# A four-layer graph network on one core: layer 0 with the adjacency as TensorE's weights

## The chip, the core and the metric

The kernel runs on one core of a Trainium2 chip, in one launch. The metric is the device time of that launch in microseconds. A core has TensorE (matmuls, out of weights that are loaded ahead of each of them, into PSUM), VectorE (DVE), ScalarE (ACT) and GpSimd (POOL), and queues that issue DMA transfers; here the SyncE queue (SP) issues nearly all of them.

## The reference, cut to what matters

A graph of 4096 nodes has features x (4096 x 64) and a dense float32 adjacency `adj` (4096 x 4096) of zeros and ones, 67 MB. Four layers follow one another, each as `x = layernorm(x + layer(x, adj))`. Layers 1 and 3 are hyperbolic attention over all pairs of nodes, layer 2 a decayed sum over each node's last neighbours. The change is in layer 0:

```
deg = clip(sum(adj, axis=1) + 1, 1)
h_neigh = (adj @ X + X) / deg
z = concat([X, h_neigh], axis=1) @ W + b          # W: 128 x 64
out = relu(z);  out = out / max(norm(out), 1e-12)
x = layernorm(x + out)
```

So z is X W_top + b + ((adj + I) X W_bottom) / deg: multiplying by W_bottom can come after the sum over neighbours or before it.

## The kernel before, in words

The host lays the adjacency out as (group of target nodes, source node within its block, block of source nodes, target node). There are four groups of 1024 targets (`GROUPS`, worked from 3 down to 0) and 32 blocks of 128 source nodes (`BLOCKS`, 31 down to 0). `load` (L712) brings two blocks for one group: 128 x 2048 float32, 1 MB, into one of six buffers. As the entries are 0 or 1, the upper half of each float32 is the same number in bfloat16; `edge` is that view, with a step of two elements. Every layer streams the adjacency again, 64 loads each.

*Layer 0, before.* `parts_of` (L1489 to L1492) splits x into three bfloat16 parts whose sum is x: two of 64 columns each side by side in `first`, the last in `third` together with a column of ones. For each block of source nodes, these parts are TensorE's weights (128 or 65 columns), and the edges are the moving operand, 512 targets at a time (L1602): four matmuls per block, so eight per load. The sums have features on partitions and targets along the row, in four PSUM banks of a group: two for `first`, two for `third`. The identity term is added by 16 small matmuls per group (L1611). At the end of a group the four accumulators are copied to SBUF, L1628 and L1636, on ScalarE (for the last group two of them on VectorE). `end_0` then multiplies them in float32 by W_bottom with the three parts added up (L1541 by `sum_w`, L1546 by `count_w`, which also passes the count of neighbours); this turns targets onto partitions. After that come the division by the degree (L1551 to L1553), the node's own part (L1554), relu (L1558), squares on POOL (L1560) and the norm (L1562 on). The own part x W_top + b is computed by `linear` (transposes L1396, a copy L1401, products L1407) and `own_part` (L1527), one group later.

*Checks.* `check` (L876) on VectorE makes sure that a load holds zeros and ones alone; it reads the whole load and so holds its buffer. In layer 0 between five and seven of the 16 loads of a group are checked, the others in layer 2.

*Order of the work.* Work per group that isn't the big stream (ends of groups, norms, preparation of the next layer's operands in `norm_rows` and `prepare`) is written as Python generators, "row work". `tick(n)` advances a counter and emits those steps of the queues whose due count has come; `later` puts a generator into a queue, and `yield n` asks for n ticks. `need(tag)` emits steps until a tag is done. So a step's place in the program is set by ticks. In layers 0 and 2 the order on TensorE and ScalarE is the program's (`manual_schedule`), elsewhere the tile scheduler chooses the order by readiness that it estimates, within what `in_order` (a dependency without a semaphore) fixes. `mark` ties row work behind the last pair instruction of its engine, but not while `anchored[0]` is false, as it is in the first group of a layer.

*Layer 1 and 3.* `attend` works one group against all 32 blocks, two blocks to a load. For each block: six matmuls into a z tile of two PSUM banks (L1170, L1173, L1176), a sigmoid (L1133) and a square (L1190) on ScalarE, a product on VectorE (L1193); for each two blocks a second product on VectorE (L1196) and eight float32 passes on TensorE (L1148). There are three z tiles, in the banks that layer 0's accumulators had. In the first pass of layer 1 (group 3), the row work of the last group of layer 0 (group 0) runs beside the pairs, much of it on POOL: L1560, the inverse roots (L784 to L795), L1566 and L1567, then `norm_rows` from L929.

Of the kernel before, what the change touches and what calls it, by code (L numbers as in the profile page):

```python
# [10 lines left out]
F32 = mybir.dt.float32  # L11
F16 = mybir.dt.float16
I32 = mybir.dt.int32
BF16 = mybir.dt.bfloat16
# [5 lines left out]
P = 128  # L20
# [41 lines left out]
def gnn_stack_kernel(  # L62
# [4 lines left out]
    weights: bass.AP,  # L67
    small: bass.AP,
# [14 lines left out]
    given_b = const.tile([P, 2 * D + 3], F32, name="given_b")  # L83
    nc.scalar.dma_start(given, small[:, : 2 * D + 3])
# [479 lines left out]
    def stream(fits):  # L564

        with ExitStack() as st:
# [307 lines left out]
            def check(s, g, a, junk):  # L874
                n = s * (NB // 2) + g
                V.scalar_tensor_tensor(  # L876
                    junk, a, 0.0, a, ALU.not_equal, ALU.not_equal, accum_out=odd[:, n : n + 1]
                )
# [247 lines left out]
            def sigmoid(layer, s, j):  # L1126
# [6 lines left out]
                nc.scalar.activation(sig, left_bs[s], AF.Sigmoid, bias=right[:, j : j + 1])  # L1133
                return sig

            def attend(layer, s, rate, then):
# [4 lines left out]
                lag = []  # L1141
# [14 lines left out]
                for g in reversed(range(NB // 2)):  # L1156
# [4 lines left out]
                    for k in (1, 0):  # L1161
# [27 lines left out]
                        sig = ahead_of.pop() if ahead_of else sigmoid(layer, s, j)  # L1189
                        nc.scalar.activation(  # L1190
                            sq[:, k], zp, AF.Square, bias=ROOT + OFF, scale=-1.0 / UNIT
                        )
                        V.scalar_tensor_tensor(ts[k][:, k], zp, 0.0, sig, ALU.max, ALU.mult)  # L1193
                        tick(rate)
# [194 lines left out]
            def linear(layer, s, weights, finish):  # L1389

                for h in range(2):
                    xt = row.tile([P, W], F32, name="x_t")[:D]
                    yield from free()
                    t = take(F32, P, W)
                    for k in range(SB):
                        nc.tensor.transpose(  # L1396
                            t[:D, k * P : (k + 1) * P],
                            x_of(layer)[:, s * WB + h * SB + k, :], ident,
                        )
                    yield near()  # L1400
                    nc.scalar.copy(xt, t[:D])  # L1401
                    held.pop()
                    yield near()
                    yield from free()
                    t = take(F32, P, SB, D)
                    for k in range(SB):
                        nc.tensor.matmul(  # L1407
                            t[:, k, :], xt[:, k * P : (k + 1) * P], weights, start=True, stop=True
                        )
                    yield near()  # L1410
                    finish(slice(s * WB + h * SB, s * WB + (h + 1) * SB), t)
                    held.pop()
                    yield 1

# [55 lines left out]
            with ExitStack() as lp:  # L1470
                own = lp.enter_context(tc.tile_pool(name="m0_own", bufs=1))
                ps = lp.enter_context(tc.tile_pool(name="m0_ps", bufs=6, space=PSUM))
# [5 lines left out]
                first = own.tile([P, NB, 2 * D], BF16, name="first")  # L1478
                third = own.tile([P, NB, D + 1], BF16, name="third")
                xw = halves.bitcast(F32)  # L1480
                sum_w = keep.tile([P, D + 1], F32, name="sum_w")
                count_w = keep.tile([D + 1, D + 1], F32, name="count_w")
                ident_b = own.tile([P, P], BF16, name="ident_b")

                def parts_of(s):

                    at, rest = blocks(s), grp("w_att")
                    nc.sync.dma_start(x0[:, at, :], x_in[:, at, :])
                    V.tensor_copy(first[:, at, :D], x0[:, at, :])  # L1489
                    V.tensor_sub(rest, x0[:, at, :], first[:, at, :D])  # L1490
                    V.tensor_copy(first[:, at, D:], rest)  # L1491
                    V.tensor_sub(third[:, at, :D], rest, first[:, at, D:])  # L1492

                def constants():
# [10 lines left out]
                    V.memset(sum_w[:, D:], 0.0)  # L1505
                    V.tensor_copy(sum_w[:D, :D], weights_sb[:D, 1])
                    V.tensor_copy(sum_w[D:, :D], w0_sb[D:, :])
                    V.memset(count_w, 0.0)
                    V.memset(count_w[D:, D:], 1.0)
                    V.tensor_copy(count_w[:D, :D], sum_w[:D, :D])  # L1510
# [8 lines left out]
                V.memset(third[:, :, D : D + 1], 1.0)  # L1519
                parts_of(GROUPS[0])  # L1520
# [4 lines left out]
                def own_part(at, t):  # L1525

                    V.tensor_add(xw[:, at, :], t, b0_sb[:, None, :].to_broadcast([P, SB, D]))  # L1527

                def end_0(s, tops):
                    z = grp("z0")  # L1530
                    yield from free()

                    for some in ((0, 1),) if spare else ((0,), (1,)):
                        ts = []
                        for h in some:
                            top, low = tops[h]
                            t = take(F32, P, SB, P)
                            for k in range(SB):
                                cols = slice(k * P, (k + 1) * P)
                                to = t[:, k, : D + 1]  # L1540
                                one = nc.tensor.matmul(  # L1541
                                    to, top[:, cols], sum_w, start=True, stop=False
                                )
                                if place[0] == 1 and not k:
                                    in_order(one.ins, pairs_last[mybir.EngineType.PE])
# [392 lines left out]
```

## Time and profile before

| | us |
|---|---|
| median of three runs | 1046.84 (1044.62 to 1047.78) |
| the profiled execution | 1045.84 |
| its span, first to last instruction | 1043.7 |
| first layer-0 matmul | 9.33 |
| last two layer-0 matmuls (L1602) begin | 173.41 |
| first pair matmul of layer 1 (L1170) | 177.12 |
| first L1196 of layer 1's first pass | 183.97 |
| first L1196 of its second pass | 273.96 |

The granted TensorE clock is 0.986 of full speed on average.

In a timeline line the columns are: start, duration, engine, line of the kernel, operation, output and input by the program's names, shapes, how many instructions are merged, and in brackets the idle time before it with what ended that. PE is TensorE's matmuls, PEld its loads of weights. A float32 matmul shows as two instructions (two passes).

### The profile page before, as it was taken

To read this page: it belongs to the slowest core of one execution; us is meant where nothing else is said; L and a number is where in the kernel's file an instruction comes from. 1 tells how busy PE (TensorE), PEld (TensorE's weight loads), DVE (VectorE), ACT (ScalarE), POOL (GpSimd) and SP (SyncE) were. 2 spreads that over 40 slices of the span, in tenths; PEclk is the share of its full clock that TensorE was granted. 3 is DMA by queue.
4 is the path that set the end of the run, shared out by engine and by line. 5 is a ranking of instruction groups with operands and counts; after the bars stand their busy time and mean duration, and the time that the engine had idled before them with its cause. 6 is when DMAs were issued, how large, how long until landed. Compare 5 with 4: busy or idle time off the path is not lost.

```text
span 1043.7 us, 13511 instructions
## 1 busy us (share of the span) xinstructions
PE 969.8 (93%) x4759; PEld 397.0 (38%) x4845; DVE 906.7 (87%) x1404; ACT 751.8 (72%) x872; POOL 332.5 (32%) x695
## 2 busy tenths in 40 slices
PE   6899999899999999999999999998999999999991
PEld 2455455333333333333333344443333333333320
DVE  7485876799999999999489489979999999999996
ACT  0103125679989898898677688898998898888960
POOL 0011111471066256266111020105402652562660
PEclk9999999899999999999999999999999999999996
DMA  9999999655675566566599999995565665665600
GB/s 370 420 413 421 369 421 421 230 174 189 223 249 214 202 235 212 197 237 216 227 346 349 374 348 322 317 335 197 201 218 192 237 241 194 243 219 200 214 8 17
DMA packets 38242, 271.62 MB, mean 260 GB/s; under 512 B 4242, under 2 KB 4371, under 8 KB 5396
## 3 DMA queue, kind: packets, MB, share of 16 engines
q1 hardware_dynamic: 37728, 270.03, 70.3%
q8 instruction: 40, 0.66, 0.2%
q10 hardware_dynamic: 436, 0.63, 0.2%
q14 instruction: 38, 0.31, 0.1%
HBM read 269.58 MB, written 1.05 MB: 259 GB/s over the span
## 4 chain that ended last, share of the span: by engine, by line
PE 56%; DVE 15%; POOL 5%; ACT 4%; issue 2%; ACTq 0%; POOLq 0%; DVEq 0%
PE acc L1148 16%; PE z L1790 11%; PE z L1173 7%; PE z L1176 7%; PE z L1170 7%; DVE t L1196 7%; DVE t L1193 6%; PE z L1802 3%; PE z L1756 2%; ACT sq L1190 1%; ACT sq L1797 1%; PE aux L1279 1%; PE aux L1114 1%; ACT sig L1133 1%; POOL rb L969 0%
## 5 line engine op out<-in xcount | busy, mean ns | idle before, releaser
L1193 DVE SCALAR_TENSOR_TENSOR t<-z,sig 128x1024 f32<-128x1024 f32 x255 | 307.3, 1217 | 17.2 <-ACT sq L1190 15.0
L1190 ACT ACTIVATE sq<-z 128x1024 f32<-128x1024 f32 x256 | 255.2, 1023 | 59.2 <-PE z L1176 27.8
L1196 DVE SCALAR_TENSOR_TENSOR t<-sq,t 128x2048 f32<-128x2048 f32 x127 | 294.4, 2318 | 0.3
L1133 ACT ACTIVATE sig<-left_b,right 128x1024 f32<-128x1024 f32 x255 | 286.1, 1150 | 10.4 <-DVE t L1193 6.2
L1148 PE MATMUL acc<-t,xe 128*64 128x512 f32 x1024 | 255.9, 609 | 11.7 <-DVE t L1196 11.4
L1173 PE MATMUL z<-lo_hi,hi_lo 128*128 128x512 f16 x512 | 194.2, 379 | 3.6 <-issue 0.7
L1176 PE MATMUL z<-dst,src 74*128 74x512 f16 x512 | 195.3, 381 | 0.0
L1170 PE MATMUL z<-edges,two_i 128*128 128x512 bf16 x462 | 181.4, 393 | 7.8 <-DVE t L1193 5.6
L1797 ACT ACTIVATE sq<-z 128x512 bf16<-128x512 f32 (+1 forms) x192 | 138.1, 740 | 39.4 <-PE z L1790 38.5
L1148 PEld LDWEIGHTS acc<-t,xe 128*64 128x64 f32 x1024 | 64.0, 136 | 141.3 <-issue 105.8
L876 DVE SCALAR_TENSOR_TENSOR t<-edges 128x2048 bf16<-128x2048 f32 x41 | 94.0, 2308 | 18.8 <-DMA edges<-in_adj_dram 18.8
L1170 PEld LDWEIGHTS <-two_i 128*128 128x128 bf16 x512 | 50.2, 98 | 120.8 <-issue 74.7
L1602 PE MATMUL acc<-edges,first 128*128 128x512 bf16 x241 | 76.9, 395 | 16.9 <-DVE first L1491 9.3
L1790 PE MATMUL z<-edges,pass_by 128*128 128x512 bf16 x241 | 84.8, 388 | 6.7 <-ACT sq L1797 5.8
L1790 PE MATMUL z<-edges,enter 128*128 128x512 bf16 x247 | 85.4, 387 | 0.4
L1602 PE MATMUL acc<-edges,third 128*65 128x512 bf16 x256 | 79.7, 392 | 0.6
L1176 PEld LDWEIGHTS <-src 74*128 74x128 f16 x512 | 49.2, 96 | 72.4 <-issue 10.9
L1173 PEld LDWEIGHTS <-hi_lo 128*128 128x128 f16 x512 | 50.3, 98 | 62.9 <-issue 17.4
L876 DVE SCALAR_TENSOR_TENSOR junk<-edges 128x2048 bf16<-128x2048 f32 x23 | 52.5, 2284 | 15.0 <-DMA edges<-in_adj_dram 15.0
L1296 POOL TENSOR_TENSOR w_att<-x,u 128x512 f32<-128x512 f32 x6 | 16.2, 2706 | 149.4 <-ACT u L1290 149.4
L1401 ACT COPY x_t<-aux 64x512 f32<-64x512 f32 x8 | 4.6, 576 | 64.4 <-PE aux L1396 64.4
L1560 POOL TENSOR_TENSOR sq<-z 128x512 f32<-128x512 f32 x4 | 10.0, 2491 | 122.2 <-DVE z L1558 101.5
(477 smaller groups left out, 1034.5 us busy)
## 6 DMA issues: line engine op xcount, KB each, us to landing
edges<-in_adj_dram SPq DMA_DIRECT2D x256, 1024.0 KB, 5.0
x<-in_x_dram SPq DMA_DIRECT2D x4, 256.0 KB, 8.8
out_dram<-x ACTq DMA_DIRECT2D x2, 256.0 KB, 2.4
out_dram<-x SPq DMA_DIRECT2D x2, 256.0 KB, 2.4
weights_sb<-in_weights_dram ACTq DMA_DIRECT2D x1, 96.0 KB, 6.2
given<-in_small_dram ACTq DMA_DIRECT2D x1, 0.5 KB
xw<-in_small_dram ACTq DMA_DIRECT2D x1, 2.0 KB
```

Of the source, the lines that this page charges most:

```text
L876: V.scalar_tensor_tensor(junk, a, 0.0, a, ALU.not_equal, ALU.not_equal, accum_out=odd[:, n : n + 1])
L1133: nc.scalar.activation(sig, left_bs[s], AF.Sigmoid, bias=right[:, j : j + 1])
L1148: it = nc.tensor.matmul(acc[h * D : (h + 1) * D, :], xe[:, j, :], t[:, k, h * W : (h + 1) * W], start=j == BLOCKS[0], stop=j == BLOCKS[-1],)
L1170: nc.tensor.matmul(half, two_i, edge[:, at : at + W], start=True, stop=False)
L1173: nc.tensor.matmul(half, hi_lo[:, of], lo_hi[:, to], start=False, stop=False)
L1176: last = nc.tensor.matmul(half, src[:, of], dst[:, to], start=False, stop=True)
L1190: nc.scalar.activation(sq[:, k], zp, AF.Square, bias=ROOT + OFF, scale=-1.0 / UNIT)
L1193: V.scalar_tensor_tensor(ts[k][:, k], zp, 0.0, sig, ALU.max, ALU.mult)
L1196: V.scalar_tensor_tensor(t, sq, HIGH**2, t, ALU.add, ALU.mult)
L1602: nc.tensor.matmul(accs[h][:m], lhs[:, j, :], edge[:, at : at + W], start=j == BLOCKS[0], stop=j == BLOCKS[-1],)
L1790: nc.tensor.matmul(z[:, h : h + W], lhs, rhs[:, h : h + W], start=j == BLOCKS[0], stop=True, skip_group_check=True,)
L1797: weighed[0] = nc.scalar.activation(w, z[:, :n], AF.Exp, bias=-(OFF_EDGE + CUT) * LN2, scale=-LN2)
```

## The change

W_bottom is applied before the sum over neighbours. For each half group (four blocks), `turn` transposes x, and the new `parts_of` multiplies it by a 65 x 128 matrix `enter_w` that the host puts together (W_bottom beside W_top, with b as its last row against a row of ones). The first 64 columns of the product are split into three bfloat16 parts, and these lie side by side with a column of ones in `parts`, 193 columns; the other 64 are the own part `xw`. Then the two operands change places: a 128 x 128 piece of the edges is TensorE's weights, and the 193 columns are the moving operand. A load takes 16 matmuls of 193 columns, each with its own weights. The sums have targets on partitions, two blocks of targets to a bank, four banks to a group, six banks in rotation (`BANKS`). At the end of a group VectorE adds the three parts up from PSUM and takes reciprocals of the counts. `linear`, `own_part`, `sum_w`, `count_w`, the copies of the accumulators and the float32 products of `end_0` go.

x comes in four pieces within the first loads (`fetch`) rather than one per group. Some orders are fixed by hand: the checks of the first group behind the first split, the split of the second layer's weights behind the second one, the norm's reduce of the last group behind the last pair operation, and four sigmoids of the first pass behind squares. The last group's `end_0` waits in ticks of other counts.

```diff
+    enter_w = const.tile([D + 1, 2 * D], F32, name="enter_w")
+    nc.scalar.dma_start(enter_w, enter_in)
...
-                nc.scalar.activation(sig, left_bs[s], AF.Sigmoid, bias=right[:, j : j + 1])
+                one = nc.scalar.activation(sig, left_bs[s], AF.Sigmoid, bias=right[:, j : j + 1])
+                if 1 < len(squares) < 6:
+                    in_order(one.ins, squares[-2].ins)
...
+                def turn(h):
+                    t = bank(4).rearrange("p b f -> p (b f)")
+                    for k in range(SB):
+                        nc.tensor.transpose(
+                            t[:D, k * P : (k + 1) * P], x0[:, h * SB + k, :], ident
+                        )
+                    nc.scalar.copy(x_ts[h % 2][:D], t[:D])
...
+                    for k in range(SB):
+                        nc.tensor.matmul(
+                            t[:, k, :], x_ts[h % 2][:, k * P : (k + 1) * P], enter_w,
+                            start=True, stop=True,
+                        )
+                    rest = grp("w_att")[:, :SB, :]
+                    hi, mid, lo = (parts[:, at, n * D : (n + 1) * D] for n in range(3))
+                    V.tensor_copy(hi, t[:, :, :D])
+                    V.tensor_sub(rest, t[:, :, :D], hi)
+                    nc.scalar.copy(xw[:, at, :], t[:, :, D:])
+                    V.tensor_copy(mid, rest)
+                    split.append(V.tensor_sub(lo, rest, mid))
...
+                def end_0(s, total, deg):
+                    z, pooled = grp("z0"), s == GROUPS[-1]
+                    yield 2 if pooled else 1
+                    V.tensor_mul(z, total, over(deg))
+                    V.tensor_add(z, z, xw[:, blocks(s), :])
                     V.tensor_scalar(z, z, 0.0, None, ALU.max)
                     sq, n2 = grp("sq"), nums("n2")
                     nc.gpsimd.tensor_mul(sq, z, z)
-                    yield 1
-                    V.tensor_reduce(n2, sq, AX.X, ALU.add)
+                    yield 2 if pooled else 1
+                    one = V.tensor_reduce(n2, sq, AX.X, ALU.add)
+                    if pooled:
+                        in_order(one.ins, pairs_last[mybir.EngineType.DVE])
...
-                                for lhs, accs, m in parts:
-                                    for h in range(2):
-                                        at = k * WW + h * W
-                                        nc.tensor.matmul(
-                                            accs[h][:m], lhs[:, j, :], edge[:, at : at + W],
-                                            start=j == BLOCKS[0], stop=j == BLOCKS[-1],
-                                        )
+                            for i in range(WB):
+                                for k in (1, 0):
+                                    j = 2 * g + k
+                                    at = k * WW + i * P
+                                    nc.tensor.matmul(
+                                        banks[i // 2][:, i % 2, :PARTS], edge[:, at : at + P],
+                                        parts[:, j, :PARTS],
+                                        start=j == BLOCKS[0] and i % 2 == 0, stop=j == BLOCKS[-1],
+                                        skip_group_check=True,
+                                    )
...
+                        for q in (0, 2, 3, 1) if last else range(4):
+                            acc = banks[q]
+                            at = slice(2 * q, 2 * q + 2)
+                            V.tensor_reduce(
+                                total[:, at],
+                                acc[:, :, : 3 * D].rearrange("p b (c d) -> p b d c", c=3),
+                                AX.X, ALU.add,
+                            )
+                            V.reciprocal(deg[:, at], acc[:, :, 3 * D])
                         if not last:
-                            later(end_0(s, tops))
-                        if s > 0:
-                            own_of = linear(0, s - 1, w0_sb[:D, :], own_part)
-                            later(in_turn((0, s - 1), own_of))
+                            later(end_0(s, total, deg))
...
-                        later(end_0(GROUPS[-1], tops), False, 4)
+                        later(end_0(GROUPS[-1], total, deg))
```

## The prediction

> **What bounds the kernel now.** I read the page first (busy shares, then the 40 slices), then windows of 4 us over layer 0, the queue's own waits, and the timelines of TensorE, ScalarE and VectorE around the step from layer 0 to layer 1. The first two pieces are from the page, the third from the windows (us; PE, PEld, DVE, ACT, POOL busy; clock; DMA share; GB/s), the fourth from the DMA queue's waits between 60 and 175 us (sum, times, longest).
>
> ```profile
> PE 969.8 (93%) x4759; PEld 397.0 (38%) x4845; DVE 906.7 (87%) x1404; ACT 751.8 (72%) x872; POOL 332.5 (32%) x695
> ...
> DMA  9999999655675566566599999995565665665600
> ```
>
> ```profile
> 88.00:92.00 4.00, 3.84 (x28) 2.18 (x28) 0.20 (x1) 2.36 (x4) 0.00 (x0) 1.00 0.99 414
> ...
> 116.00:120.00 4.00, 3.94 (x20) 1.81 (x19) 3.93 (x19) 0.00 (x0) 0.00 (x0) 1.00 0.90 344
> 120.00:124.00 4.00, 4.00 (x32) 2.27 (x31) 3.83 (x11) 1.35 (x3) 0.00 (x0) 1.00 0.89 326
> ```
>
> ```profile
> SPq L712 <- DVE junk L876: 50.1, 15, 5.8
> ```
>
> A slice is 26.1 us, and the seven full slices of DMA are layer 0. There 64 loads of 1.05 MB arrive at 421 GB/s, 2.49 us each. TensorE looks full, but its work on a load is 8 matmuls at 0.226 us, 1.8 us; it is not the bound of this stage. What layer 0 loses is at most the dip between 112 and 132 us: 365, 344, 326, 334 and 397 GB/s where 421 is possible, worth (56+77+95+87+24) x 4 / 421 = 3.2 us. VectorE is full there, still working off its checks (L876, 2.28 us, which hold the load's buffer) and row work.
>
> After layer 0, pairs (layers 1 and 3) take 4.6 us for two blocks on VectorE (2 x 1.14 + 2.2) and nearly that on TensorE. From the step itself, TensorE:
>
> ```profile
> 173.86 0.61 PE L1030 MATMUL aux<-ident,ys 128*128 128x128 f16 x8
> ...
> 177.12 0.39 PE L1170 MATMUL z<-edges,two_i 128*128 128x512 bf16 x1 [2.21 <-ACT w_att L1636]
> ...
> 179.76 0.33 PE L1541 MATMUL acc<-sum_w,sums 128*128 128x65 f32 x2
> ...
> 183.28 0.39 PE L1170 MATMUL z<-edges,two_i 128*128 128x512 bf16 x1
> ```
>
> TensorE stands 2.21 us until ScalarE has emptied the accumulators, does two blocks of pairs, and then spends 3.52 us on the 32 float32 passes of `end_0`. VectorE, same region:
>
> ```profile
> 179.97 1.23 DVE L1193 SCALAR_TENSOR_TENSOR t<-z,left_b 128x1024 f32<-128x1024 f32 x1 [4.62 <-ACT sq L1190]
> 181.70 0.18 DVE L1551 RECIPROCAL deg<-acc 128x4 f32<-128x4 f32 x1 [0.50 <-PE acc L1546]
> ...
> 203.08 0.69 DVE L929 TENSOR_REDUCE n_m<-z 128x8 f32<-128x512 f32 x1 [4.00 <-POOL z L1567]
> ```
>
> The first pass of layer 1 is poor: 16 double blocks take 90.0 us between their L1196 (183.97 to 273.96), against 16 x 4.6 = 73.6.
>
> **Matmuls of layer 0.** Removed per load: 8 matmuls of 512 columns. Added: 16 of 193 columns, each with a new 128x128 weight. No row has a weight read with a step of two bfloat16. The nearest is L1030: eight float16 weights of 128x128 and eight matmuls of 128 columns take 0.61 us with the last one's latency of 0.22, so 0.056 us a pair: loading hides. Then 193 columns cost 193/2.4 + 2.5 ns = 83 ns (512 columns: 216 ns in the pairs, the same form), or 16 x 83 = 1.33 us a load. The other end: float32 weights (twice the bytes per column, as the step here) in L1541 take 0.111 us a pair. That makes 1.78 us. [...] I take 1.33: type and width are the row's. All three lie below the 2.49 us of a load, so TensorE's gain is worth only what is left after the last load: at most 1.80 - 1.33 = 0.5 us. The diagonal becomes 8 x 83 = 0.7 us for 0.9 (0.2 less, off the path).
>
> **The product x W, moved ahead.** For each of eight half groups: 4 float32 transposes (0.11 us each), a copy on ScalarE (0.58), 4 float32 products, 4 VectorE steps. This replaces `parts_of` (0.42+0.69+0.42+0.69 = 2.2 us per group of 8 blocks) and `linear`; VectorE's four steps on half the elements, partly from PSUM, come to about 1.35 us, 10.9 us in all against 8.9 + 3.3 (L1527). It falls in group 3, where VectorE later stands for 4 and 7 us, so zero. At the start: x at 4.3 us, transposes 0.7, copy 0.6, product 0.7, parts 1.35, handovers 0.5: about 8.2 us to the first edge matmul instead of 9.33; if the new weight arrives only when `weights_sb` does (7.6), 10.1. Neither counts: six buffers fill until about 18 us, and TensorE works faster than loads arrive. x's own loads are the same bytes, in front of the edges' loads by 0.4 us of issue each on SP's queue; the small load of W delays two others on ScalarE's queue by 0.5 us. The checks now stand behind the first parts, at 8 to 10 us, where the first check already starts at 10.07.
>
> **Emptying the sums.** Instead of four copies (0.58 us each on ScalarE; in the last group two of them on VectorE), VectorE makes four reduces over 384 elements and four reciprocals. Reduces: 0.203 us for 48 elements from PSUM (L1057), 0.683 for 512 (L1562), so 1.03 ns an element and 0.55 us for 384; with 0.18 for a reciprocal, 4 x 0.73 = 2.9 us. [...] I keep the row's 0.55. Behind them wait the next group's third and fourth pair of columns (TensorE has over 1 us of slack per load), its checks and row work. At the ends of groups 3 and 2 VectorE is idle (it waits 9.08 us before 91.8 for a load), so the reduces mostly lie in idle time. Removed behind them: 2.9 us of VectorE (L1551, L1553, L1554, L1527) and a wait of 1.46 us on TensorE's float32 sums; added: two operations of 0.69. In group 1, where VectorE is full from 94 to 129 us, this leaves 2.9 + 1.46 - 1.38, minus 0.7 of reduces that reach into the group = 2.3 us less lag, and buffers come back that much sooner. Of the 3.2 us dip this can recover between 0 and 2.3; value 1.5, since row chains also wait on POOL.
>
> **The step to layer 1.** The last load lands near 171.85 (the one before it was waited for at 169.36, plus 2.49). Its matmuls end at 173.2 instead of 173.86. The 16 transposes of row work (0.9 us) follow, to 174.1; the first load of layer 1 lands at 174.3. The reduces start when the first bank is done, before the last matmul, so the first z tile is free by 173.7, or by 175 if all four come first. First pair matmul: 174.6 instead of 177.12, 2.5 us. ScalarE also loses its 0.95 us of copies ahead of the first Square, so L1193 at 179.97 follows by as much.
>
> **The first pass.** TensorE's 3.52 us of float32 sums go. VectorE bounds here, and its part (2.04 us, a wait of 0.50, 0.42) becomes 1.38 + 0.42: 0.7 us. The later row waits stay or move: a 0.93 us wait for POOL's square before the norm is now arranged two ticks apart and behind a pair's operation; between 0 and 0.9, value 0.5. The 4.00 us wait at L929 plus the double block that follows at a lower clock (6.24 instead of 4.6) is 5.6 us: it can go (-5.6), stay (0), or another like it come (+5.6), since VectorE's order in this pass isn't fixed. That code isn't edited, so 0. The new order of four sigmoids behind squares costs at most one 1.15 us and is ahead of VectorE; 0. The rest of the row chain of the last group starts some 7 us earlier and so doesn't become late. Layers 2 and 3 only shift.
>
> **Sum.** 1.5 (dip) + 2.5 (first pair) + 0.7 + 0.5 = 5.2, with 0.3 of ScalarE's early start: 5.5 us. The profiled execution took 1045.84 (span 1043.7 and 2.1 around it), so 1040.3; the median of the runs shown is 1.0 above it: 1041.3, rounded to 1041.
>
> **Rivals.**
> - *Gains are larger*: the 4 us wait goes too, 1041 - 5.6 = 1035. For: its chain starts earlier. Against: nothing edited in it. 0.16.
> - *Given back in the first pass*: VectorE is put behind one more wait for POOL; 1041 + 5.6 = 1046.6. For: the unfixed order, POOL's operations of 2.2 us where 0.2 is usual. 0.20. With two such waits, 1052: 0.09.
> - *Loads of weights don't hide* (slower): the stepped weight is loaded one after the other with the matmul, [...] It decides from 2.49/16 = 156 ns a pair. Against: both rows hide it. 0.05.
> - *Nothing reaches the end* because layer 0 is the DMA's: dip and waits unchanged, 1041 + 4 = 1045; contained in the second.
>
> **Chances.** The likeliest, 0.50, lies between 1038 and 1043.7. About 0.3% is what a measurement of this kernel can tell: 1043.7 to 1050.0 is "same". Faster 0.50 + 0.16 = 0.66, same 0.20, slower 0.14. The range 1034 to 1049 leaves out the two slower cases and the ends of the two others.
>
> **What would show it.** Layer-0 matmuls at about 83 ns; DMA above 400 GB/s from 112 to 132 us; the first pair matmul 2 to 3 us earlier, with no float32 sums behind the second block; the last group's square on POOL near 182 instead of 189.67; 16 double blocks of the first pass in 87 to 90 us. Wrong if a pair of weight and matmul takes over 156 ns, if VectorE's reduces hold up the first z tile, or if the pass gains waits.

## The result and the profile after

| | before | after |
|---|---|---|
| median, us (lowest to highest) | 1046.84 (1044.62 to 1047.78) | 1035.30 (1034.48 to 1035.77) |
| the profiled execution / its span | 1045.84 / 1043.7 | 1035.30 / 1033.6 |
| last layer-0 load: its matmuls begin | 172.05 | 168.07 |
| first pair matmul of layer 1 | 177.12 | 170.98 |
| first two-block product of VectorE in layer 1 | 183.97 | 176.82 |
| first such product of the second pass | 273.96 | 263.36 |

The ratio is 0.9894, with a 95% interval of 0.988 to 0.9909: 1.1% faster. 1041.0 was forecast. The last four rows show where the 10.6 us come from: 4.0 in the stream of layer 0, 2.15 at the handover to layer 1 (6.14 at the first pair), 1.0 until VectorE's first two-block product (7.15), and 3.45 in the first pass (10.6). From there to the end of the span 0.5 us is given back. These are differences of two single profiles, and the stream's part scatters: run 2 below leaves layer 0 as it was, and its first pair still comes 0.92 us earlier than in the profile of the kernel before. Line numbers shift by a few: L1602 became L1584, L1193 and L1196 became L1198 and L1203, the check L876 became L879, the load L712 became L715.

The page after, busy shares and the DMA row of the 40 slices, and further down the two groups of the new layer-0 line (busy us, mean ns | idle before, released by):

```profile
PE 940.1 (91%) x5197; PEld 417.9 (40%) x5197; DVE 910.2 (88%) x1420; ACT 747.0 (72%) x866; POOL 333.9 (32%) x695
...
DMA  9999999655666566575799998995465666665500
...
L1584 PE MATMUL acc<-parts,edges 128*128 128x193 bf16 x1024 | 100.2, 252 | 37.8 <-DMA edges<-in_adj_dram 37.0
...
L1584 PEld LDWEIGHTS <-edges 128*128 128x128 bf16 x1024 | 86.7, 100 | 48.5 <-DMA edges<-in_adj_dram 46.4
```

TensorE lost 30 us of busy time, and at the edge matmuls it now waits 37 us for loads (6.7 before): in layer 0 the DMA is the slower of the two. That idle time costs nothing; the seven full DMA slices are still seven. Windows of 4 us after (PE, PEld, DVE, ACT, POOL busy; clock; DMA share; GB/s):

```profile
88.00:92.00 4.00, 2.97 (x39) 2.64 (x38) 4.00 (x11) 1.57 (x2) 0.00 (x0) 1.00 1.01 426
...
116.00:120.00 4.00, 2.88 (x33) 2.46 (x31) 3.97 (x8) 1.66 (x3) 0.10 (x1) 1.00 0.89 330
120.00:124.00 4.00, 1.89 (x21) 1.44 (x18) 3.69 (x19) 0.00 (x0) 2.33 (x7) 1.00 0.98 344
```

Two things are to be seen. Of the dip only the stretch from 116 to 124 is left, (96 + 82) x 4 / 426 = 1.7 us instead of 3.2. And the rate where nothing holds the loads is 426 instead of 421 GB/s (414 in the same window before), which the prediction did not foresee. The DMA queue's own waits, 60 to 175 us:

```profile
SPq L715 <- DVE junk L879: 54.2, 14, 6.6
SPq L715 <- PE acc L1584: 28.9, 24, 2.8
```

The longest wait for a load's buffer is still for a check on VectorE. The handover, TensorE and then VectorE (timelines):

```profile
165.59 1.53 PE L1584 MATMUL acc<-parts,edges 128*128 128x193 bf16 x16 [0.91 <-DMA edges<-in_adj_dram]
...
168.07 1.51 PE L1584 MATMUL acc<-parts,edges 128*128 128x193 bf16 x16
169.43 0.61 PE L1033 MATMUL aux<-ident,yd 128*74 128x128 f16 x8
170.98 0.39 PE L1175 MATMUL z<-edges,two_i 128*128 128x512 bf16 x1 [0.95 <-DVE deg L1623]
```

```profile
168.61 0.56 DVE L1618 TENSOR_REDUCE sums<-acc 128x128 f32<-128x384 f32 x1 [3.16 <-PE acc L1584]
...
170.61 0.23 DVE L1623 RECIPROCAL deg<-acc 128x2 f32<-128x2 f32 x2
170.87 0.69 DVE L1532 TENSOR_TENSOR z<-sums,deg 128x512 f32<-128x512 f32 x1
171.60 0.69 DVE L1533 TENSOR_TENSOR z<-z,halves 128x512 f32<-128x512 f32 x1
172.33 0.43 DVE L1534 TENSOR_SCALAR z<-z 128x512 f32<-128x512 f32 x1
173.61 1.23 DVE L1198 SCALAR_TENSOR_TENSOR t<-z,left_b 128x1024 f32<-128x1024 f32 x1 [0.85 <-ACT sq L1195]
...
176.82 2.29 DVE L1203 SCALAR_TENSOR_TENSOR t<-sq,t 128x2048 f32<-128x2048 f32 x1
...
189.44 0.69 DVE L932 TENSOR_REDUCE n_m<-z 128x8 f32<-128x512 f32 x1 [2.87 <-POOL z L1545]
```

A load's 16 weights and matmuls take 1.52 us, and a single matmul lasts 0.25 (252 ns on the page): (1.52 - 0.25) / 15 = 0.085 us a pair. The four reduces and reciprocals end at 170.84, and the first pair follows 0.14 later. What `end_0` then does on VectorE, 1.8 us, lies in front of the first L1198, in time in which VectorE would wait for ScalarE's first Square anyway (0.85 of that wait is left). The last line is the wait for POOL before the reduce of `norm_rows`: 2.87 instead of 4.00. POOL, the last group's square before (first line) and after, then one of its small operations, and VectorE's product that runs beside that one:

```profile
189.67 2.95 POOL L1560 TENSOR_TENSOR sq<-z 128x512 f32<-128x512 f32 x1 [24.88 <-DVE z L1558]
...
172.90 1.04 POOL L1536 TENSOR_TENSOR sq<-z 128x512 f32<-128x512 f32 x1 [12.97 <-DVE z L1534]
...
183.34 2.20 POOL L793 TENSOR_SCALAR rs_t<-rs_t 128x8 f32<-128x8 f32 x1
...
183.16 2.28 DVE L1203 SCALAR_TENSOR_TENSOR t<-sq,t 128x2048 f32<-128x2048 f32 x1
```

The last group's square starts at 172.90 instead of 189.67 and takes 1.04 us instead of 2.95. The small operation, 2.20 us for eight elements a row where 0.20 is usual, has its like before (L790 at 196.97); the section on the hardware comes back to it.

### The profile page after: what moved, and what is told of

Same layout as the page of the kernel before. It is cut to its first block, busy times and chain, and to the rows that moved or that the text cites. A ratio compares the mean times of both kernels' runs of the same rounds, so it can differ in the third digit from the quotient of the medians.

```text
span 1033.6 us, 14323 instructions
## 1 busy us (share of the span) xinstructions
PE 940.1 (91%) x5197; PEld 417.9 (40%) x5197; DVE 910.2 (88%) x1420; ACT 747.0 (72%) x866; POOL 333.9 (32%) x695
## 3 DMA queue, kind: packets, MB, share of 16 engines
HBM read 269.62 MB, written 1.05 MB: 262 GB/s over the span
## 4 chain that ended last, share of the span: by engine, by line
PE 60%; DVE 20%; DMA 7%; ACT 5%; POOL 5%; issue 2%; SPq 0%; ACTq 0%; POOLq 0%; DVEq 0%
PE acc L1153 17%; PE z L1774 11%; PE z L1175 8%; PE z L1181 7%; DVE t L1203 7%; PE z L1178 7%; DMA edges<-in_adj_dram 7%; DVE t L1198 6%; PE z L1786 3%; PE z L1740 2%; DVE junk L879 2%; ACT sq L1195 2%; PE acc L1584 2%; ACT sq L1781 1%; ACT sig L1136 1%
## 5 line engine op out<-in xcount | busy, mean ns | idle before, releaser
L1198 DVE SCALAR_TENSOR_TENSOR t<-z,sig 128x1024 f32<-128x1024 f32 x255 | 307.2, 1218 | 18.7 <-ACT sq L1195 16.5
L1203 DVE SCALAR_TENSOR_TENSOR t<-sq,t 128x2048 f32<-128x2048 f32 x127 | 294.4, 2318 | 0.3
L1175 PE MATMUL z<-edges,two_i 128*128 128x512 bf16 x512 | 200.8, 392 | 2.5 <-DVE t L1198 1.5
L1584 PE MATMUL acc<-parts,edges 128*128 128x193 bf16 x1024 | 100.2, 252 | 37.8 <-DMA edges<-in_adj_dram 37.0
L879 DVE SCALAR_TENSOR_TENSOR t<-edges 128x2048 bf16<-128x2048 f32 x41 | 94.0, 2308 | 20.0 <-DMA edges<-in_adj_dram 20.0
L1584 PEld LDWEIGHTS <-edges 128*128 128x128 bf16 x1024 | 86.7, 100 | 48.5 <-DMA edges<-in_adj_dram 46.4
L1774 PE MATMUL z<-edges,pass_by 128*128 128x512 bf16 x248 | 86.5, 388 | 6.3 <-ACT sq L1781 5.7
L1774 PE MATMUL z<-edges,enter 128*128 128x512 bf16 x256 | 88.2, 387 | 0.0
L1178 PEld LDWEIGHTS <-hi_lo 128*128 128x128 f16 x512 | 50.2, 98 | 57.1 <-issue 11.5
L979 ACT CAST ys<-y 128x512 f16<-128x512 f32 x8 | 4.9, 616 | 74.3 <-DVE y L976 44.6
L879 DVE SCALAR_TENSOR_TENSOR junk<-edges 128x2048 bf16<-128x2048 f32 x23 | 52.5, 2282 | 0.0
L1740 PE MATMUL z<-sq,halves 128*128 128x512 bf16 x128 | 48.0, 377 | 0.2 <-ACT sq L1781 0.2
```

Source lines behind the costliest of these rows:

```text
L879: return V.scalar_tensor_tensor(junk, a, 0.0, a, ALU.not_equal, ALU.not_equal, accum_out=odd[:, n : n + 1])
L1175: nc.tensor.matmul(half, two_i, edge[:, at : at + W], start=True, stop=False)
L1178: nc.tensor.matmul(half, hi_lo[:, of], lo_hi[:, to], start=False, stop=False)
L1203: V.scalar_tensor_tensor(t, sq, HIGH**2, t, ALU.add, ALU.mult)
L1584: nc.tensor.matmul(banks[i // 2][:, i % 2, :PARTS], edge[:, at : at + P], parts[:, j, :PARTS], start=j == BLOCKS[0] and i % 2 == 0, stop=j ...
L1774: nc.tensor.matmul(z[:, h : h + W], lhs, rhs[:, h : h + W], start=j == BLOCKS[0], stop=True, skip_group_check=True,)
```

## The experiments

Two parts of the 10.6 us asked for a cause: the stream's 4.0, of which the dip explains 1.5, and the first pass's 3.45, of which 0.5 was forecast. For the pass the first theory was that the orders set by hand carry about 3 us; the rival, that they carry nothing and the earlier start of the last group does it. For the stream the candidates were the number of times TensorE reads an edge (twice before, as moving operand for `first` and for `third`; once after, as weight), VectorE's checks, and the place of the load buffers in SBUF. Runs are given as median (lowest to highest), and as ratio to the kernel before in the same set, with its 95% interval; the kernel before had medians of 1046.38, 1045.67 and 1046.25 in the three sets (runs 1 to 4, 5 to 8, 9 to 12).

**1. The kernel after, with the old order in the first pass.**

```diff
-                if 1 < len(squares) < 6:
-                    in_order(one.ins, squares[-2].ins)
...
-                    yield 2 if pooled else 1
+                    yield 1
...
-                    if pooled:
-                        in_order(one.ins, pairs_last[mybir.EngineType.DVE])
...
-                        later(end_0(GROUPS[-1], total, deg))
+                        later(end_0(GROUPS[-1], total, deg), False, 4)
```

> The changed kernel with the order of the first pass of layer 1 put back: end_0 of the last group waits four ticks, its two yields are 1, the norm's reduce and the four sigmoids are not tied to anything. Theory (hand-set order carries the pass): first pass about 90 us again instead of 86.5, time 1038 to 1039. Rival (what counts is that the float32 sums and copies are gone): pass 86 to 87.5, time 1035 to 1036.

Measured: 1034.63 (1033.86 to 1035.48), ratio 0.989 (0.9874 to 0.9907), the same as the kernel after. The first theory fell. VectorE's timeline shows why:

```profile
174.06 0.69 DVE L1536 TENSOR_REDUCE n<-sq 128x8 f32<-128x512 f32 x1 [1.22 <-POOL sq L1534]
...
178.47 2.83 DVE L1201 SCALAR_TENSOR_TENSOR t<-sq,t 128x2048 f32<-128x2048 f32 x1
...
186.94 0.68 DVE L932 TENSOR_REDUCE n_m<-z 128x8 f32<-128x512 f32 x1
```

Without the hand-set order VectorE waits 1.22 us for POOL before the norm, and its first two-block product comes 1.65 us later (178.47 for 176.82). In return POOL's chain has ended early enough that the wait before `n_m` is gone, and the pass takes 83.9 us instead of 86.5. The second pass starts at 262.41, 0.95 before that of the kernel after; the second pass gives it back (the third starts at 339.01, in the kernel after at 339.08), and nothing of it is left in the time.

**2. The kernel before, with its last `end_0` put earlier** (2 ticks instead of 4, and the norm behind the last pair operation).

```diff
-                    yield 1
-                    V.tensor_reduce(n2, sq, AX.X, ALU.add)
+                    yield 2 if s == GROUPS[-1] else 1
+                    one = V.tensor_reduce(n2, sq, AX.X, ALU.add)
+                    if s == GROUPS[-1]:
+                        in_order(one.ins, pairs_last[mybir.EngineType.DVE])
...
-                        later(end_0(GROUPS[-1], tops), False, 4)
+                        later(end_0(GROUPS[-1], tops), False, 2)
```

> The kernel before with only the order changed: end_0 of the last group starts two ticks earlier, its norm's reduce comes two ticks after POOL's square and is tied behind the last pair operation. Theory (order alone brings it): the waits of VectorE for POOL (0.93 and 4.00 us) shrink, first pass 86 to 88 us, time 1043 to 1044.5. Rival (the order is good only together with the turned layer 0): pass 89 to 91 us, time within 1 us of before.

Measured: 1051.41 (1047.17 to 1054.87), ratio 1.005 (1.0034 to 1.0067): 5 us slower, which no expectation named. TensorE's first pair, then VectorE:

```profile
176.20 0.39 PE L1170 MATMUL z<-edges,two_i 128*128 128x512 bf16 x1 [2.21 <-ACT w_att L1638]
...
181.61 0.18 DVE L1551 RECIPROCAL deg<-acc 128x4 f32<-128x4 f32 x1 [7.19 <-PE acc L1546]
...
184.97 0.18 DVE L1551 RECIPROCAL deg<-aux 128x4 f32<-128x4 f32 x1 [1.25 <-PE aux L1546]
```

The 32 float32 passes now stand behind the first block of pairs, and VectorE's first two-block product comes at 190.06 instead of 183.97. But the granted clock in this profile is 0.50 from 177 to 190 us, where that of the kernel before has 1.00 (a matmul of 512 columns takes 0.63 us instead of 0.38, and they start 0.43 us apart instead of 0.22), and how much of the 5 us that makes is not shown. What the run shows: with the float32 sums on TensorE, VectorE waits for them when the last group's end is put early (7.19 and 1.25 us here, at half the clock), and nothing is gained. The change takes that wait away. Layer 0 is unchanged in this run, and its first pair comes at 176.20, in the profile of the kernel before at 177.12: so far apart can two executions of the same stream be.

**3. The kernel before, with half of TensorE's layer 0.**

```diff
-                                for lhs, accs, m in parts:
+                                for lhs, accs, m in parts if j in (BLOCKS[0], BLOCKS[-1]) else parts[:1]:
```

> The kernel before with the matmuls of the third part and of the counts left out for all but the first and last block, so its sums are incomplete and only its time is read: TensorE needs 0.9 us a load, and reads each edge once instead of twice. Theory (the DMA is slowed by TensorE's reads of the edges, and the dip near 112 to 132 us is VectorE's): 424 to 427 GB/s while the stream is full instead of 421, and the dip of some 3 us stays; about 2 us faster than before. Rival 1 (rate is the chip's or the run's): 421 stays. Rival 2 (the dip is TensorE's lag): the dip goes, and with it 3 us.

Measured: 1044.93 (1043.48 to 1049.79), ratio 0.999 (0.9982 to 0.9997). Two of its windows:

```profile
80.00:100.00 20.00, 14.58 (x93) 9.20 (x95) 10.65 (x31) 9.22 (x14) 2.69 (x7) 0.83 1.01 421
...
120.00:124.00 4.00, 1.49 (x6) 0.48 (x5) 3.90 (x16) 1.09 (x3) 0.00 (x0) 1.00 0.87 328
```

TensorE is busy for 1.49 of 4 us, and still the dip is there (328 GB/s) beside a VectorE at 3.90. From 112 to 132 us 1.7 us are lost instead of 3.2, but a stop from 72 to 76 us (246 GB/s) costs 1.7 instead of 0.4; over both, nearly as much as before (3.3 for 3.7). So the stops are not TensorE's, and its work in layer 0 is worth at most the 1.5 us of this run. The full rate is 421, although edges are read half as often.

**4. The kernel after, with four more reads of the edges per load as moving operand, in groups 2 and 1.**

```diff
+                            if not last and s != GROUPS[0]:
+                                for h in range(4):
+                                    nc.tensor.matmul(
+                                        spare_bank, ident_b, edge[:, h * W : (h + 1) * W],
+                                        start=True, stop=True, skip_group_check=True,
+                                    )
```

> The changed kernel with four more matmuls per load in groups 2 and 1 that read the whole load once more as moving operand into a bank that nobody reads. TensorE needs 1.35 + 0.9 = 2.25 us a load, still under 2.49. Theory (reads slow the DMA): 420 to 423 GB/s in groups 2 and 1 (about 50 to 128 us), 426 in the others; 1 us slower than the changed kernel. Rival (the rate has another reason): 426 everywhere, time 1035.3 within 0.5.

Measured: 1035.64 (1034.53 to 1036.69), ratio 0.9898 (0.9881 to 0.9914), and 421 to 428 GB/s in the windows of 10 us from 50 to 130 us outside the dip, where the reads are (424 to 428 in run 1, which lacks them). With run 3: how often TensorE reads the edges makes no difference to the rate here.

**5 and 6. 64 bytes per partition put ahead of the load buffers, in the kernel after and in the kernel before.** The buffers lie where the tiles allocated ahead of them end. The change adds 512 bytes there (`enter_w`) and removes 520 (`sum_w`, `count_w`), and after rounding the buffers start at byte 93952 of each partition instead of 94016. 93952 is a multiple of 256, 94016 is 64 more than one.

```diff
+            pad = keep.tile([P, 16], F32, name="pad")
+            V.memset(pad, 0.0)
             hi_lo = keep.tile([P, N], F16, name="hi_lo")
```

> The changed kernel with 64 unused bytes per partition put ahead of its buffers. The build places the six load buffers of the kernel before at 94016 bytes and on in a partition, 64 above a multiple of 128, those of the changed one at 93952, a multiple of 128; this puts them at 94016. Theory (the place of the buffers sets the DMA's rate, and the rise from 421 to 426 GB/s is no merit of the turned matmuls): 421 GB/s in layer 0, first pair matmul 1.9 us later, time about 1037. Rival (the rate has another cause): 426, 1035.3 within 0.5.

> The kernel before with the same 64 bytes, which put its load buffers at 94080, a multiple of 128. Theory: 426 GB/s instead of 421 in layer 0, layer 1 starts some 1.9 us earlier, time 1044.5 to 1045. Rival: 421 and no difference.

Measured, after with the pad (start 94016): 1036.49 (1035.72 to 1037.69), ratio 0.9908 (0.9891 to 0.9924). First pair at 172.39, 1.4 us later than without, although its dip costs only 0.7 us. Its windows:

```profile
20.00:40.00 20.00, 19.14 (x200) 18.24 (x199) 17.49 (x74) 3.39 (x8) 0.00 (x0) 1.00 1.01 419
...
132.00:165.00 33.00, 22.28 (x263) 19.74 (x261) 30.93 (x121) 6.36 (x10) 6.58 (x9) 1.00 1.01 421
```

The same kernel with nothing but a shifted address falls back to the rate of before; run 8, of the same set and with its buffers at 93952, has 425 and 426. (The pad shifts every tile behind it. That it is the load buffers which count is argued from the rate being that of the loads into them.) Before with the pad (start 94080, a multiple of 128 but not of 256): 1045.38 (1043.83 to 1046.91), ratio 0.9993 (0.9984 to 1.0001), 419 to 423 GB/s outside the stops: no gain in the rate, though in this profile too the first pair comes early, at 175.87.

**9. The kernel before with 192 bytes instead** (`[P, 48]` in the same edit; start 94208, a multiple of 256).

> The kernel before with 192 unused bytes ahead of its load buffers, at 94208, a multiple of 256 as in the changed kernel (93952); with 64 bytes (94080, a multiple of 128 only) the rate stayed at 421. Theory (a multiple of 256 counts): 425 to 427 GB/s in layer 0, first pair matmul about 1.9 us earlier than 177.1, time 1044 to 1045. Rival (the rate belongs to the turned kernel in some other way): 421 GB/s, no difference.

Measured: 1043.40 (1042.28 to 1048.16), ratio 0.9976 (0.9962 to 0.999).

```profile
20.00:40.00 20.00, 16.97 (x77) 7.75 (x74) 17.00 (x66) 0.58 (x1) 0.00 (x0) 1.00 1.01 425
...
132.00:165.00 33.00, 31.90 (x200) 18.74 (x199) 29.73 (x112) 7.17 (x12) 6.64 (x9) 1.00 1.01 426
```

The kernel before takes on the rate of the kernel after, from its address alone; its first pair matmul comes at 174.01, 3.1 us earlier than in the profile of the kernel before and 1.9 to 2.2 earlier than in those of runs 6 and 2, with a dip of nearly the old size (2.7 us). So of the 11.5 us, 1.2 (run 5, in one direction) to 2.5 (this one, in the other; 1 to 4 by its interval) come from where the buffers happen to lie, and have nothing to do with turning the matmuls round. Run 5's 1.2 compares medians of two sets, and the intervals of the two ratios overlap: the rate is shown, its share of the time only roughly. The loads of layer 0, 67.1 MB, take 1.9 us longer at 421 GB/s than at 426.

**7 and 10. The kernel after, with 16 float32 matmuls of 65 columns put back** at the place of the old sums (their results are not used). In run 7 their operand lies ahead of the load buffers, in run 10 behind them.

```diff
+                    if pooled:
+                        t = take(F32, P, SB, P)
+                        for k in range(4 * SB):
+                            nc.tensor.matmul(
+                                t[:, k % SB, : D + 1], ident, xe_old[:, : D + 1],
+                                start=True, stop=True,
+                            )
```

> The changed kernel with 16 float32 matmuls of 65 columns (32 passes, results unused) put back into the last group's end_0 in its first step, as TensorE had them before. Theory (the pass is VectorE's, TensorE's 3.5 us are only partly felt): first pass 0.5 to 2 us longer than 86.5, time 1036 to 1037.5. Rival (the missing 3.5 us of TensorE are the gain of the pass): 3 to 4 us longer, 1038.5 to 1039.5.

> The changed kernel with the 16 float32 matmuls (32 passes) put back as before, now with their operand behind the load buffers, which stay at 93952. Theory (the pass is VectorE's): 426 GB/s, first pass 87.5 us instead of 86.5, time 1036 to 1037. Rival (the 3.5 us of TensorE are felt in full somewhere): 1038 to 1039.

Run 7: 1039.00 (1038.39 to 1039.09), ratio 0.9933 (0.9916 to 0.9949). It doesn't separate: its buffers start at 94240, 32 beyond a multiple of 256, its rate is 417 to 419 GB/s in windows of 20 and 33 us outside the dip, and the first pair comes 1.7 us late already. Run 10, with the buffers where the kernel after has them: 1036.50 (1035.90 to 1038.05), ratio 0.9905 (0.9869 to 0.9941), 424 to 426 GB/s in such windows. TensorE:

```profile
173.36 3.68 PE L1535 MATMUL acc<-xe_old,ident 128*128 128x65 f32 x32
...
176.88 0.39 PE L1175 MATMUL z<-edges,two_i 128*128 128x512 bf16 x1
```

The passes hold TensorE as long as the old ones (3.52 us, from 173.36 to the next pair at 176.88), yet the first two-block product comes no later (176.55), and the pass takes 87.48 instead of 86.54, at the same granted clock (0.86 from 188 to 200 us in both). So TensorE's 3.5 us of float32 sums are worth 0.9 us of the pass when VectorE doesn't wait for their results.

**8. The kernel after, with two checks of group 1 moved from layer 0 to layer 2.**

```diff
-                more = {0: (4, 6, 8), 1: (4,), 2: (4, 6, 8), 3: (4, 6)}
+                more = {0: (4, 6, 8), 1: (4, 6, 8), 2: (4, 6, 8), 3: (4, 6)}
```

> The changed kernel with two checks of group 1 (loads 8 and 6) moved from layer 0 to layer 2, where other checks lie. Theory (the dip left at 116 to 124 us, 1.7 us, is VectorE's checks holding buffers): the dip goes, layer 1 starts 1.5 us earlier, layer 2 takes them for nothing, time 1033.5 to 1034. Rival (layer 2 pays 2 x 2.3 us or the dip is a row chain's): 1035 to 1038.

Measured: 1045.33 (1043.23 to 1046.57), ratio 0.9992 (0.998 to 1.0003): the whole gain is lost. The same stretch of layer 0, and one of layer 2:

```profile
116.00:120.00 4.00, 2.79 (x31) 2.33 (x30) 3.11 (x14) 1.66 (x3) 2.31 (x7) 1.00 1.02 424
120.00:124.00 4.00, 2.30 (x26) 1.84 (x23) 0.00 (x0) 0.00 (x0) 0.00 (x0) 1.00 1.02 432
...
600.00:640.00 40.00, 30.25 (x158) 14.31 (x161) 38.11 (x121) 27.36 (x47) 11.53 (x15) 0.91 0.79 286
```

The dip is gone, and the first pair comes at 169.68, 1.3 us earlier: what is left of the dip is the checks', and worth 1.3 of its 1.7 us. But in layer 2 two more checks of 2.3 us meet a VectorE that was at 37.60 of these 40 us without them. TensorE does 30.25 us of work in place of 36.90, and ScalarE stands for 9.3. Layer 3 begins 10.0 us late (first two-block product at 708.23 instead of 698.19). That is more than the 4.6 us of the two checks, and the waits from 480 to 720 us show where it comes from (sum, times, longest):

```profile
PE acc L1117 <- DVE left L1073: 7.7, 1, 7.7
```

`left` (L1073) is made late in a row chain on VectorE, among the checks, and TensorE, which has this wait nowhere in layer 2 of the kernel after, stands until it is done. The granted clock is 0.91 in these 40 us and 0.96 in the next, 1.00 in both in the kernel after.

**11. The kernel after, last group emptied in another order of banks.**

```diff
-                        for q in (0, 2, 3, 1) if last else range(4):
+                        for q in (1, 3, 2, 0) if last else range(4):
```

> The changed kernel with the last group's four reduces in the order 1, 3, 2, 0, so that the banks of the first z tile come last and the bank that is finished last comes first. Theory (the first pair matmul waits for these reduces, here for all four from the end of layer 0's matmuls): first pair matmul at about 172.6 instead of 170.98, time 1036 to 1037. Rival (the first pair matmul waits for the load or for row work): 171 and no difference.

Measured: 1034.14 (1033.22 to 1035.92), ratio 0.9889 (0.9847 to 0.9931); no loss, against what was expected. TensorE:

```profile
170.49 0.39 PE L1175 MATMUL z<-edges,two_i 128*128 128x512 bf16 x1 [1.06 <-DMA edges<-in_adj_dram]
```

In both orders the first pair starts 0.1 to 0.25 us after the last reciprocal (170.84 and 170.25), and here the profile puts its wait down to the first load of layer 1. By the semaphore updates in the traces the last piece of that load lands at 170.84 in the kernel after and at 170.35 here: there the two fall together, here the load comes last. In the profiles of runs 1, 5, 7, 8, 10 and 12 the load lands 0.2 to 0.4 us before the last reciprocal ends, and the pair follows that reciprocal by 0.10 us. So all four reduces are waited for, but the load leaves at most 0.4 us to win.

**12. Run 1's order, and two checks of group 1 exchanged:** loads 8 and 6 are checked in layer 2, loads 3 and 1 in layer 0 in their place.

```diff
                 more = {0: (4, 6, 8), 1: (4,), 2: (4, 6, 8), 3: (4, 6)}
+                if s == 1:
+                    return g in (0, 2, 4, 5, 6, 7, 8, 9, 11)
```

> The changed kernel with the order of the first pass put back as in the first experiment, and two checks of group 1 exchanged: loads 8 and 6 are checked in layer 2 and loads 3 and 1 in layer 0, where VectorE stands idle, so that both layers have as many as before. Theory (the dip at 116 to 124 us is VectorE's checks, and layer 2 lost in the other experiment because it got two more): the dip goes, layer 1 starts 1.3 us earlier, layer 2 keeps its time, 1033 to 1034. Rival (where layer 2's checks lie matters, not how many): 1036 or more.

Measured: 1034.80 (1034.53 to 1034.97), ratio 0.9891 (0.9851 to 0.9932). The dip is gone (425 and 430 GB/s from 110 to 130 us) without more checks in layer 2, and the second pass starts at 261.46, 1.9 us before that of the kernel after. Yet the span ends at 1033.2 (1033.6). The second pass gives back 0.9 us (the third starts at 338.06 instead of 339.08), and in layer 2 TensorE waits 1.4 us for `left`, as in run 8. No version tried here is faster than the kernel after by more than the runs scatter.

## Why the prediction was right in direction and half the size

5.5 us were forecast and 10.6 are in the trace. By the prediction's own steps:

| step | forecast, us | measured, us | from |
|---|---|---|---|
| dip in layer 0 | 1.5 | 1.5 | windows of 4 us |
| rate of the loads | 0 | 1.4 to 1.9 | first pair of run 5; 67.1 MB at 421 and 426 GB/s |
| stream, not assigned | 0 | 0.6 to 1.1 | rest of 4.0; run 2's profile differs by 0.9 with the same layer 0 |
| first pair matmul behind the stream | 2.5 | 2.15 | 0.45 matmuls, 1.7 handover |
| ScalarE's start | 0.3 | 0.2 | VectorE's first product 2.85 and 2.63 us behind the first pair |
| VectorE's own steps | 0.7 | 1.9 | 0.8 from there to the two-block product; 1.07 in the pass, VectorE busy 80.52 to 79.45 |
| waits in the first pass | 0.5 | 2.4 | below |

- *Matmuls of layer 0: right.* 0.085 us a pair against 0.083 forecast; the line through L1030's 56 ns for 128 columns and the pairs' 216 ns for 512 gives the same 83. In the profile a load of a weight with the step is 100 ns long (L1584), one without it 98 before (L1602), and as the pairs follow each other at 85 ns, it lies beside other matmuls. The rival in which loads of weights don't hide falls with that: from 156 ns a pair it would have counted. Run 3 confirms that TensorE's speed in this stage is worth at most 1.5 us.
- *Emptying the sums: right in the reduce.* One of 384 elements took 0.54 to 0.56 us (0.55 forecast, from the rows of L1057 and L1562). All four with their reciprocals took 2.2 us, not 2.9.
- *The dip: right* in size (1.5 of 3.2). Its cause is in part shown: run 3 takes TensorE out of it, and run 8 has what is left go with VectorE's checks. That the 1.5 us came from the work taken off VectorE behind the reduces is the prediction's argument; no run put that work back.
- *The rate: wrong.* The step that failed is the first one, "64 loads of 1.05 MB arrive at 421 GB/s": it was taken as a property of the DMA. Runs 5 and 9 show that it belongs to the address of the buffers, which the change moved without meaning to. The diff had it: constants of other sizes are allocated ahead of the buffers.
- *The first pair: nearly right.* 0.45 us for the shorter matmuls (at most 0.5 forecast), 1.7 for the handover. The reading that all four reduces would hold up the first tile (175 in place of 173.7 in the sum) was the true one; it cost at most 0.4 us, as the layer's first load comes hardly earlier (run 11).
- *ScalarE's start and VectorE's own steps: right in kind, less than half the size.* ScalarE's 0.3 came as 0.2 (the text there speaks of 0.95). For VectorE the sum set 1.38 + 0.42 us of new steps against 2.04 + 0.50 + 0.42 of old ones; that is 1.16 by these figures, and its 0.7 leaves the wait of 0.50 out. And in the new kernel the 1.8 us lie in front of the first Square, where VectorE would wait: they cost nothing, and all of the old ones that stood on the path count.
- *The waits in the pass: the step that failed most.* VectorE's waits there sum to 9.3 us before and 7.0 after. The one before the norm went (0.93; 0.5 forecast), the one at `n_v`, the second reduce of `norm_rows`, went (0.93; 0 forecast), the one at `n_m`, the first, shrank from 4.00 to 2.87 (0 forecast, as "that code isn't edited"); waits for ScalarE grew by 0.6. What failed is the reason: code that isn't edited still changes its place among the pairs when its chain starts 17 us earlier. That the hand-set orders do it is refuted by run 1. Run 10 gives TensorE's sums 0.9 us of the pass. Some 0.9, an estimate from the passes that follow here, go with the clock: behind the wait for `n_m` TensorE is granted less, 0.72 on average from 200 to 212 us before, 0.86 from 188 to 200 us after. Runs 4 and 8, which leave the order of this pass alone, have 0.72 there (the next eight float32 passes take 3.68 us in both) and passes of 87.5 and 87.4 us; runs 5 and 11 have 0.86 (3.20 and 3.27 us; 1.94 at a clock of 1.00), and 86.6 and 86.3. That the rest follows from the earlier start fits the trace; no run separates it further.

The rival "gains are larger" named 1035 and so hit the time, with the wrong mechanism: it let the whole wait of `n_m` go. In run 1 that wait is gone, and the time is the same. That the measured time lies within 1034 to 1049 at all is in part luck: the likeliest stretch was 1038 to 1043.7, and 1.2 to 2.5 us came from an address that nobody chose. The first edge matmul came at 9.34, not 8.2: the first float32 transposes took 1.03 us (0.7 forecast) and the first products 2.08 (0.7 forecast); as said, nothing depends on it.

Left open: 0.6 to 1.1 us of the stream, which may be chance; what in the second pass takes back 0.9 us in runs 1 and 12; and what run 2 would cost at the full clock.

## What to carry to other kernels

Before a change is priced, look at what it moves in memory besides what it means to move: here 1.2 to 2.5 of 11.5 us were an address, and a kernel of unchanged logic could have had them. A row chain that starts earlier is worth more than its own operations if they can lie in front of the next stage's first result; set its steps against the wait that is there, not against the steps they replace. And work is not moved out of a dip that costs 1.7 us into a stage whose VectorE is full at 94% and in which TensorE waits for a row chain on it.

## What the runs showed of the hardware

- *Loads and the address of their buffer.* 1 MB loads of 8 KB per partition ran at 424 to 427 GB/s (in windows of 20 us and more outside the stops) with the buffers at bytes 93952 and 94208 of a partition (multiples of 256), and at 417 to 423 at 94016, 94080 and 94240 (64, 128 and 32 beyond one). Five addresses, no more. 421 for 426 is 1.2% less at 64, and it is about as much at 128 (419 to 423) and at 32 (417 to 419): no order by the offset. What makes the difference was not shown.
- *POOL beside VectorE.* POOL's operation of eight elements a row took 0.20 us, and 2.20 where VectorE's two-block product ran beside it: L793 above starts at 183.34 and ends at 185.54, VectorE's product, from 183.16, ends at 185.44. From 170 to 470 us of the kernel after, all 23 such operations that start while a two-block product runs take 2.15 to 2.35 us and end 0.06 to 0.21 us behind it. The last group's square, 1.04 us with no such product beside it, took 2.95 before, from 189.67 to 192.62, where such a product ran from 189.44 to 191.73. The product L1198, whose z is in PSUM, shows no such effect: in the same stretch the 220 small operations that lie wholly beside it take 0.19 to 0.33 us.
- *TensorE at the start.* Eight float32 products of 128 columns (L1493) took 2.08 us at 5.5 us into the run and 1.16 us at 25 us, 1.8 times as long. It isn't float32 alone: in the kernel before, two edge matmuls took 1.05 us at 14.43 and 0.61 at 15.78, 1.7 times as long. The traces' records of the granted clock begin at 15.4 us before and 12.6 after, with 1.00; the 1.00 that the profile gives for earlier windows has no record behind it. What slows TensorE at the start was not shown.
